# Storing each expert's outputs by index to the rows of its pairs, and the last seven tiles in one branch

## The chip, the cores and the metric

The kernel runs on one core of a Trainium2 chip. The metric is the device time of one execution in microseconds (us). Engines are named as in the profile: PE (TensorE, matrix products), DVE (VectorE), ACT (ScalarE), POOL (GpSimd) and SP (SyncE, which only issues DMAs here). POOL issues DMAs too, and all those that go by a list of row numbers (indirect ones) are issued by it.

## What is computed

One decoder layer over 4 sequences of 512 tokens with 512 features, in f32:

```
x = x + attn (layernorm(x))     # Mamba: projections, conv, selective scan, out_proj
x = x + xattn(layernorm(x))     # two int8 SmoothQuant linears per sequence
x = x + ffn  (layernorm(x))     # mixture of experts
```

The change lies in the last line. Of 16 experts each token takes its two best, with weights `topw` that add to one:

```
topw, sel = top_k(softmax(x @ gate_w.T), 2);  topw /= topw.sum(-1)
combine[t, sel[t]] = topw[t]
hmid = silu(x @ w1[e].T) * (x @ w3[e].T)              # 128 wide
moe_out = sum over e of combine[:, e] * (hmid @ w2[e].T)
out = moe_out + sigmoid(x @ shared_gate.T) * shared(x)
```

So each token has two pairs (token, expert), and its result is the shared part plus two weighted rows.

## The kernel before, in words

**Order of the work.** Most of the time goes to the scan: 256 units, each with `bu` on POOL (L726), `da` on ACT (L724), the scan itself and `h` on DVE (L733, L739) and sums on PE (L751). Beside the units of later batches run the `backs`: for each sequence out_proj, layernorm (L377 to L395), the two quant linears (`amx` and `s` on POOL at L927 to L930) and `moe_front` (layernorm, router, shared expert). The sequences form two groups of two, and `experts` (L1240) does the routed part of one group. Group 0 begins beside the scan of the last sequence, group 1 when that sequence has been routed, after the scan.

Every piece of such work is a generator that yields what it waits for. While the kernel is written out, a planner, `Pace` (L133 to L245), keeps a model of each engine's time with fixed costs and lets a piece go on beside the scan only if the model says that nothing of the scan is held up (`clear`, L222). After the scan the piece goes first whose wait is ready first (`run`). Each engine then executes its own instructions strictly in the order written out; so does SP's and POOL's queue with their DMAs.

**One group of experts.** A group has 1024 tokens, thus T = 8 token tiles of 128 and 2048 pairs. `sort` (L1354) orders the pairs by expert and lays them out in tiles of 128 rows, each tile of one expert only. At most NS = 2T + 16 - 1 = 31 tiles are needed; 16 always are (`sure`), 24 are called `likely`, and the number for the given data is in `count`. `sort` leaves three index tables: `tok`, the token row of each place in a tile (out of bounds where it is empty), `wrow`, the weight rows of each tile's expert, and `pos`, the place of each token's two pairs.

`expert_tiles` (L1475) goes through the tiles. `load` has POOL gather the tile's rows, `xs` (L1507, 256 KB), and its expert's weights, `wx` (L1263, 768 KB). `steps` then are: four transposes on PE (L400), a copy to `xT` on ACT (L1529), 16 products (L1538), Tanh on ACT (L1544), two operations on DVE (L411, L1548), the product with w2 (L1553), a copy to `ys` on ACT (L1557), and a plain store of the tile by SP to its own 128 rows of `y_d` (L1561). Up to 8 tiles are loaded ahead after the scan, 2 during it; three are in work at a time. `load` of tile s+8 is written out when tile s has ended.

For tiles that may not be needed, `part` (L1483) puts each single step into a branch of the engine that does it. For tiles 16 to 23 only the two products are in a branch, with a small product as the other way; for tiles 24 to 30 every step but the loads is, on every engine, SP's store among them. The branch reads `count`:

```
if s < sure or s < likely and out is None: yield; return
...
with self.tc.If(counts[engine] > s) as real: yield
```

**The sums.** At the end of a group, for each of the 8 token tiles: SP fetches the rows of the residual with the shared part, `xr4` (L1278, 256 KB; for group 1 all eight are fetched by `some` when the last tile's loads are written out), POOL gathers the two `yg` by `pos` from `y_d` (L1301), DVE multiplies by `topw` and adds, twice (L1311), and SP stores to `out` (L1318). Rows of `y_d` above the likely tiles are filled from `x` once, during the scan (`first_experts`, L1672), since nothing else may have written them.

Of the kernel before, what the change touches and what calls it, by code (L numbers as in the profile page):

```python
# [8 lines left out]
F32 = mybir.dt.float32  # L9
# [10 lines left out]
P = 128  # L20
B = 4
L = 512
# [110 lines left out]
class Pace:  # L133
# [23 lines left out]
    def take(self, ins):  # L157
        outs = [x for x in ins.outs if hasattr(x, "bass_ap")]
        ins_ = [x for x in ins.ins if hasattr(x, "bass_ap")]
        e = str(ins.engine).rsplit(".", 1)[-1]  # L160
        if not outs or e not in self.engine:
            return
        n = 1
        for _, size in list(outs[0].ap)[1:]:
            n *= size
        kind = type(ins).__name__
        keys, outs_ = [self.key(x) for x in ins_], [self.key(x) for x in outs]
        start = max([self.engine[e]] + [self.written.get(k, 0) for k in keys])
        if e != "SP":
            start = max([start] + [max(self.written.get(k, 0), self.read.get(k, 0)) for k in outs_])  # L170
        if "DMA" in kind:
            end = start + (950 if e == "Pool" else self.FIXED[e])
            size = 1
            for _, x in outs[0].ap:
                size *= x
            self.queue = max(self.queue, end) + size * 4 / 220
            self.engine[e], done = end, max(self.queue, end + 1000) + 1000
        else:
            if e == "PE":
                cost = 40 + self.product(n / 4 if outs[0].ap[0][1] == CH else n, ins_[0].dtype == F32)  # L180
            else:
                cost = self.FIXED[e] + n * self.EACH[e] * (2 if getattr(ins, "is_tensor_tensor_scan", False) else 1)
            if e == "Activation" and kind == "InstActivation":
                table = self.TABLES.get(str(ins.func).rsplit(".", 1)[-1], self.table)
                if table != self.table:
                    cost += 1280
                    self.table = table
            self.engine[e] = start + cost
            done = self.engine[e] + self.HOP
        for k in keys:  # L190
            self.read[k] = max(self.read.get(k, 0), done)
        for k in outs_:
            self.written[k] = done
# [76 lines left out]
class Kernel:  # L270
    def __init__(self, ctx, tc, args):
        self.tc, self.nc = tc, tc.nc
        for name, ap in args.items():
# [35 lines left out]
        self.y_d = [  # L309
            self.dram.tile([(2 * n * NT + E - 1) * P, DM], F32, name=f"y_d{i}") for i, (_, n) in enumerate(GROUPS)  # L310
        ]
# [7 lines left out]
        self.started = set()  # L319
# [920 lines left out]
    def experts(self, sb, group, bank, ahead):  # L1240
# [13 lines left out]
        pos = sb.tile([P, T, 2], U32, name=f"pos{group}", bufs=1)  # L1254
# [17 lines left out]
        yield from self.sort(sb, bank, group, fixed, pos, tok, wrow, count, lambda: [weights(s) for s in range(ahead)], min(ahead, 3))  # L1272
        y_d = self.y_d[group]
        xr = {}
# [11 lines left out]
        yield from self.expert_tiles(group, place, bank, NS, tok, ws, count, weights, some, self.xn_d[group], y_d)  # L1286
# [5 lines left out]
        def load(t):  # L1292
            if t not in xr:
                fetch(t)
            if sb is self.last:
                both = sb.tile([P, 2, DM], F32, name="yg", tag="wx")
                ys[t] = [both[:, i, :] for i in range(2)]
            else:
                ys[t] = [self.us.tile([P, DM], F32, name="yg", tag="u") for i in range(2)]
            for i in range(2):  # L1300
                nc.gpsimd.indirect_dma_start(  # L1301
                    out=ys[t][i],
                    out_offset=None,
                    in_=y_d,
                    in_offset=bass.IndirectOffsetOnAxis(ap=pos[:, t, i : i + 1], axis=0),
                )
            return *ys[t], xr[t]
# [15 lines left out]
    def sort_fixed(self, sb, group):  # L1323
# [18 lines left out]
        tokf = iota("tokf", [[P, T]], 0, 1)  # L1342
# [11 lines left out]
    def sort(self, sb, G, group, fixed, pos, tok, wrow, count, first_weights, few):  # L1354
# [78 lines left out]
        nc.vector.tensor_copy(pos, posf)  # L1433
# [10 lines left out]
        for t in range(0, T, 2):  # L1444
# [17 lines left out]
                tokf[:, t : t + 2].rearrange("p (a b q) -> p a b q", b=1, q=1).to_broadcast([P, 2, 2, NS]),  # L1462
# [8 lines left out]
        nc.vector.tensor_add(tok, pk, none)  # L1471
# [3 lines left out]
    def expert_tiles(self, group, place, bank, NS, tok, ws, count, weights, some, xn_d, y_d):  # L1475
# [4 lines left out]
        counts = {}  # L1480

        @contextmanager
        def part(s, engine, out=None, n=1):  # L1483

            if s < sure or s < likely and out is None:
                yield
                return
            if engine not in counts:  # L1490
                counts[engine] = engine.value_load(count)
            with self.tc.If(counts[engine] > s) as real:
                yield
                inside = list(nc.cur_bb.bb.instructions)
            if s < likely:
                with real.Else():
                    some = self.identb.unsqueeze(1).to_broadcast([P, n, P])
                    nc.tensor.matmul(
                        out.rearrange("p (n q) -> p n q", n=n), self.identb, some, start=True, stop=True
                    )  # L1500
            self.pace.update()
            for ins in inside:
                self.pace.take(ins)
# [14 lines left out]
        def steps(s):  # L1518
# [5 lines left out]
            with part(s, nc.tensor):  # L1524
                self.transposes(tp, xs[s], NK)
            yield ACT, tp
            xT = sb.tile([P, NK, P], F32, name="xT", bufs=few)
            with part(s, nc.scalar):
                nc.scalar.copy(xT, tp)  # L1529
# [4 lines left out]
            with part(s, nc.tensor, ph.rearrange("p i q -> p (i q)"), 2):  # L1534
# [8 lines left out]
            with part(s, nc.scalar):  # L1543
                nc.scalar.activation(h, ph[:, 0, :], AF.Tanh, scale=0.5)  # L1544
            yield h
            with part(s, nc.vector):
                self.swish(h, h, ph[:, 0, :])
                nc.vector.scalar_tensor_tensor(h, h, 0.5, ph[:, 1, :], ALU.mult, ALU.mult)  # L1548
# [3 lines left out]
            with part(s, nc.tensor, py, NK):  # L1552
                nc.tensor.matmul(py, h, w[:, W2:], start=True, stop=True)  # L1553
            yield ACT, py
            y = sb.tile([P, DM], F32, name="ys", bufs=min(ahead, 6))
            with part(s, nc.scalar):
                nc.scalar.copy(y, py)  # L1557
            bank.done(py)
            yield SP, y
            with part(s, nc.sync):  # L1560
                nc.sync.dma_start(y_d[s * P : (s + 1) * P, :], y)  # L1561
# [3 lines left out]
        while ended < NS:  # L1565
            while loaded < NS and loaded - ended < place()[1]:
                load(loaded)
                loaded += 1
            self.done.add(("begun", group))
            if loaded == NS:  # L1570
                some()
# [7 lines left out]
            if one.over:  # L1579
                going.remove(one)  # L1580
                ended += 1

# [84 lines left out]
    def first_experts(self):  # L1667
        yield lambda: "pool" in self.done

        for y_d, (_, n) in zip(self.y_d, GROUPS):  # L1670
            rest = y_d[(2 * n * NT + E // 2) * P :, :]
            self.nc.sync.dma_start(rest, self.x.rearrange("b l d -> (b l) d")[: rest.shape[0], :])  # L1672
            yield SP
# [135 lines left out]
```

## Time and profile before

| What | Value |
|---|---|
| five runs: median, lowest, highest | 1635.13, 1628.33, 1638.32 us |
| the profiled execution: its own time | 1630.59 us |
| its span in the trace | 1628.9 us |
| mean granted PE clock | 0.849 |
| busy: PE, DVE, POOL, ACT | 1196.2, 1197.1, 1125.5, 941.1 us |
| `bu` on POOL (L726) | 256 times 2358 ns |
| `wx` gathers on POOL (L1263) | 62 times 1023 ns |
| `xs` gathers on POOL (L1507) | 62 times 1038 ns |
| `yg` gathers on POOL (L1301) | 32 times 1032 ns |
| additions on DVE (L1311) | 32 times 752 ns |
| `y_d` stores by SP | 48, of 256 KB each |

The span runs from the first to the last instruction of the profiled execution; its own time is 1.7 us longer. That execution is one of its own, so its time is compared with the runs' median only as a whole. No engine is busy for more than 73% of the span, because the stages have different limits: the scan runs until about 1338 us, the last sequence's quant linears until about 1441, then come its router, the sort of group 1 and the group's tiles, and from about 1586 the sums. The 48 stores are 24 in each group: the branches of tiles 24 to 30 were not taken, in either group.

A group of instructions is named by line, engine and "out<-in". A wait is named by what ended it; "issue" is time in which an engine waited for nothing that the profile shows. The copies to `ys` (L1557) mark the ends of tiles.

### The profile page before, as it was taken

The page shows a single profiled execution, that of the slowest core. Times are in us where ns is not written, and L with a number is a line of the kernel's source. Part 1 is how long each engine was busy: PE and PEld are TensorE (multiplying, and loading weights), DVE is VectorE, ACT ScalarE, POOL GpSimd, SP SyncE. Part 2 cuts the span into 40 slices and gives each one's busy share as a digit, 9 for nine tenths or more (in the row PEclk, how much of TensorE's full clock was granted, in tenths as well). Part 3 has the DMA queues.
Part 4 walks back from the last instruction along what each step waited for, and adds up shares of the span by engine and source line. Part 5 has one row for each costly group of instructions (what it writes and reads, how often), then busy time and mean ns, then how long its engine had stood idle before and what let it go on. Part 6 is the DMA issues. An engine that isn't in the chain of part 4 may idle for free. (4 is left out here: it accounts for less than half of the span.)

```text
span 1628.9 us, 15724 instructions
## 1 busy us (share of the span) xinstructions
PE 1196.2 (73%) x4544; PEld 584.3 (36%) x4552; DVE 1197.1 (73%) x1256; ACT 941.1 (58%) x1592; POOL 1125.5 (69%) x935
## 2 busy tenths in 40 slices
PE   5867777557865767899867885856767799868990
PEld 2323222112332323333423432334434346644770
DVE  4588999898868888788787888977788863444312
ACT  3386776755667778555797753377676323630240
POOL 1079899886768888676887965687778654316564
PEclk9977888779887887999878888987787999968995
DMA  5476555675233655666344559665556557257976
GB/s 199 146 184 131 131 113 113 127 191 115 80 85 79 137 123 151 172 181 169 82 99 118 158 125 274 161 179 142 143 147 184 142 189 265 78 194 272 362 277 219
DMA packets 109658, 262.22 MB, mean 161 GB/s; under 512 B 16192, under 2 KB 20416, under 8 KB 109504
## 3 DMA queue, kind: packets, MB, share of 16 engines
q1 hardware_dynamic: 93120, 204.50, 47.9%
q0 software_dynamic: 16448, 56.65, 9.8%
q8 instruction: 40, 0.66, 0.2%
q14 instruction: 50, 0.41, 0.1%
HBM read 168.55 MB, written 45.88 MB: 132 GB/s over the span
## 5 line engine op out<-in xcount | busy, mean ns | idle before, releaser
L726 POOL TENSOR_TENSOR bu<-bc,rep 128x1024 f32<-128x1024 f32 x256 | 602.1, 2358 | 178.4 <-DVE da L733 133.2
L733 DVE TENSOR_TENSOR_SCAN da<-da,bu 128x1024 f32<-128x1024 f32 x256 | 586.2, 2290 | 88.5 <-POOL bu L726 55.6
L724 ACT ACTIVATE da<-rep,a_sb 128x512 f32<-128x512 f32 x512 | 352.6, 690 | 249.2 <-DVE h L739 221.4
L739 DVE TENSOR_TENSOR h<-da,bc 128x1024 f32<-128x1024 f32 x256 | 312.3, 1220 | 18.9 <-PE py L751 8.7
L751 PE MATMUL py<-h,sel 128*32 128x512 f32 x1024 | 163.8, 679 | 49.0 <-DVE h L739 49.0
L1263 POOL DMA_INDIRECT wx<-in_wexp,wrow x62 | 63.4, 1023 | 73.1 <-PE bank L1553 25.1
L502 POOL TENSOR_TENSOR u<-u,tap 128x511 f32<-128x511 f32 (+2 forms) x72 | 91.2, 1266 | 17.0 <-ACT tap L498 14.7
L446 PE MATMUL bank_a<-xnT,win 128*128 128x512 f32 x176 | 96.7, 701 | 8.3 <-ACT tap L498 5.6
L446 PE MATMUL bank_g<-xnT,win 128*128 128x512 f32 x184 | 90.8, 639 | 7.4 <-ACT tap L498 4.2
L751 PEld LDWEIGHTS py<-h,sel 128*32 128x32 f32 x1024 | 30.9, 118 | 159.9 <-issue 82.0
L1507 POOL DMA_INDIRECT xs<-xn_d,tok x62 | 64.4, 1038 | 21.0 <-issue 15.1
L446 PE MATMUL bank_b<-xnT,win 128*128 128x512 f32 x120 | 60.5, 651 | 13.0 <-ACT sp_r L681 10.9
L446 PEld LDWEIGHTS bank_a<-xnT,win 128*128 128x128 f32 x176 | 39.1, 231 | 60.8 <-issue 50.0
L446 PEld LDWEIGHTS bank_g<-xnT,win 128*128 128x128 f32 x184 | 36.6, 206 | 59.8 <-issue 43.7
L1538 PE MATMUL bank<-xT,wx 128*128 128x128 f32 x384 | 49.5, 288 | 1.9 <-ACT xT L1529 1.9
L695 POOL TENSOR_TENSOR sp_e<-sp_e,dd 128x512 f32<-128x512 f32 x31 | 39.4, 1272 | 16.4 <-ACT dd L690 16.2
L1538 PEld LDWEIGHTS bank<-xT,wx 128*128 128x128 f32 x384 | 47.4, 202 | 5.3 <-ACT xT L1529 2.9
L1301 POOL DMA_INDIRECT yg<-y_d,pos x32 | 33.0, 1032 | 18.6 <-DMA y_d<-ys 9.1
L1311 DVE SCALAR_TENSOR_TENSOR xr<-yg,topw,xr 128x512 f32<-128x512 f32 x32 | 23.8, 752 | 28.0 <-DMA yg<-y_d,pos 27.6
L411 DVE SCALAR_TENSOR_TENSOR hs<-hs,bank 128x128 f32<-128x128 f32 x24 | 6.9, 286 | 51.0 <-ACT hs L1544 49.7
L446 PEld LDWEIGHTS bank_b<-xnT,win 128*128 128x128 f32 x120 | 24.7, 213 | 48.7 <-issue 30.2
L693 ACT ACT_TABLE_LOAD x32 | 41.1, 1283 | 0.5
(434 smaller groups left out, 2387.2 us busy)
## 6 DMA issues: line engine op xcount, KB each, us to landing
rep<-dd SPq DMA_DIRECT2D x128, 512.0 KB, 8.1
win<-in_win SPq DMA_DIRECT2D x64, 256.0 KB, 3.0
x<-xr SPq DMA_DIRECT2D x48, 256.0 KB, 2.0
xr<-x SPq DMA_DIRECT2D x48, 256.0 KB, 4.7
y_d<-ys SPq DMA_DIRECT2D x48, 256.0 KB, 4.2
bc<-rows_d SPq DMA_DIRECT2D x32, 256.0 KB, 5.7
gz_d<-gz SPq DMA_DIRECT2D x32, 256.0 KB, 3.4
gzl<-gz_d SPq DMA_DIRECT2D x32, 256.0 KB, 3.5
```

Of the source, the lines that this page charges most:

```text
L446: nc.tensor.matmul(pj, win[:, k, :], xnT[:, k, :], start=(k == 0), stop=(k == NK - 1))
L502: nc.gpsimd.tensor_add(u[:, j:], u[:, j:], v[j][:, j:])
L693: nc.scalar.activation(w, w, AF.Ln)
L695: ew.tensor_sub(e, e, du)
L724: nc.scalar.activation(da[:, i, :], rep[:, i, 0, :], AF.Exp, scale=self.a_sb[:, q, g : g + 1])
L726: nc.gpsimd.tensor_mul(bu, st["bc"][0, g].unsqueeze(1).to_broadcast([P, NP, L]), rep[:, :, 1, :])
L733: self.nc.vector.tensor_tensor_scan(daf, daf, buf, 0.0, ALU.mult, ALU.add)
L739: self.nc.vector.tensor_mul(h, st["da"].pop((c, n)), st["bc"][1, g].unsqueeze(1).to_broadcast([P, NP, L]))
L751: nc.tensor.matmul(py[q * CH : (q + 1) * CH, :], self.sel, st["h"][c, g, q // NP][:, q % NP, :], start=False, stop=(g == NG - 1),)
L1263: nc.gpsimd.indirect_dma_start(out=ws[s], out_offset=None, in_=self.wexp, in_offset=bass.IndirectOffsetOnAxis(ap=wrow[:, s : s + 1], axis= ...
L1507: nc.gpsimd.indirect_dma_start(out=xs[s], out_offset=None, in_=xn_d, in_offset=bass.IndirectOffsetOnAxis(ap=tok[:, s : s + 1], axis=0), bo ...
L1538: nc.tensor.matmul(ph[:, i, :], w[:, o : o + P], xT[:, k, :], start=(k == 0), stop=(k == NK - 1))
```

## The change

The change has five parts.

1. The sort now computes with the number of a pair (token times 2, plus 0 or 1) where it computed with the token. Its end makes two tables from it: `pair` (out of bounds where a place is empty) and `tok` by halving. `pos` is not kept. Five small DVE operations stand where one stood.
2. `y_d` is smaller, with a row for each pair. A tile's result is stored by POOL with an indirect DMA, to the rows of `pair`; places out of bounds are not stored. The scatters are declared independent of one another.
3. The sums read plain rows: SP loads `yg`, for group 1 both rows of 128 tokens in one DMA of 512 KB, for group 0 in two of 256 KB. Each of these loads waits for all scatters of its group. POOL's gathers go.
4. The loop goes over the 24 likely tiles. The other seven stand after it in one branch of all engines, loads included, and the fetch of `xr4` comes after that. Of the branches on single steps those around the products of tiles 16 to 23 stay.
5. The fill of `y_d` from `x` goes, and the planner's model knows the scatter (950 ns of POOL, 256 KB of queue).

In the order written out after the change, POOL has 24 scatters more per group, 14 loads of tiles 24 to 30 and 16 gathers fewer. After the scan its order per tile is the scatter of tile s, then `xs` and `wx` of tile s+8. Beside the scan stand 11 scatters, and 2 loads fewer. At the end of the branch that isn't taken POOL waits for all its DMAs.

```diff
@@ Pace.take
+        scattered = "DMA" in kind and e == "Pool" and outs_[0][0].startswith("y_d")
+        if e != "SP" and not scattered:
...
+            if scattered:
+                size = P * DM
@@ __init__
-            self.dram.tile([(2 * n * NT + E - 1) * P, DM], F32, name=f"y_d{i}") for i, (_, n) in enumerate(GROUPS)
+        self.y_d = [self.dram.tile([2 * n * L, DM], F32, name=f"y_d{i}") for i, (_, n) in enumerate(GROUPS)]
@@ experts
+        y_of = y_d.rearrange("(t p i) d -> t p i d", p=P, i=2)
...
-            for i in range(2):
-                nc.gpsimd.indirect_dma_start(
-                    out=ys[t][i],
-                    out_offset=None,
-                    in_=y_d,
-                    in_offset=bass.IndirectOffsetOnAxis(ap=pos[:, t, i : i + 1], axis=0),
-                )
+            loads = [(both, y_of[t])] if sb is self.last else [(ys[t][i], y_of[t, :, i, :]) for i in range(2)]
+            for to, of in loads:
+                ins = nc.sync.dma_start(to, of)
+                for other in self.scattered[y_d.tensor.name]:
+                    info = mybir.DependencyInfo(mybir.DependencyClass.Sync, mybir.DependencyReason.DATA)
+                    self.tc.add_manual_dep(ins.ins, other.name, info, reason="all pairs are there")
@@ sort_fixed and sort
-        tokf = iota("tokf", [[P, T]], 0, 1)
+        tokf = iota("tokf", [[2 * P, T], [1, 2]], 1, 2)
...
-        nc.vector.tensor_copy(pos, posf)
...
-        nc.vector.tensor_add(tok, pk, none)
+        nc.vector.tensor_scalar(ex, pk, 0.5, float(4 * T * P), ALU.is_lt, ALU.mult)
+        nc.vector.scalar_tensor_tensor(pair, pk, -1.0, ex, ALU.add, ALU.add)
+        nc.vector.tensor_scalar(ex, pk, -1.5, 0.5, ALU.add, ALU.mult)
+        nc.vector.tensor_scalar(ex, ex, MAGIC, -MAGIC, ALU.add, ALU.add)
+        nc.vector.scalar_tensor_tensor(tok, ex, 0.0, none, ALU.max, ALU.add)
@@ expert_tiles
-            yield SP, y
-            with part(s, nc.sync):
-                nc.sync.dma_start(y_d[s * P : (s + 1) * P, :], y)
+            yield POOL, y
+            ins = nc.gpsimd.indirect_dma_start(
+                out=y_d,
+                out_offset=bass.IndirectOffsetOnAxis(ap=pair[:, s : s + 1], axis=0),
+                in_=y,
+                in_offset=None,
+                bounds_check=2 * rows - 1,
+                oob_is_err=False,
+            )
+            for other in self.scattered.setdefault(y_d.tensor.name, []):
+                self.tc.declare_no_dep(ins.ins, other, reason="a pair has one place")
+            self.scattered[y_d.tensor.name].append(ins.ins)
...
-        while ended < NS:
-            while loaded < NS and loaded - ended < place()[1]:
+        while ended < likely:
+            while loaded < likely and loaded - ended < place()[1]:
...
-            if loaded == NS:
-                some()
...
+        yield "PE", bank.free
+        with self.tc.If(nc.values_load(count) > likely):
+            for s in range(likely, NS):
+                load(s)
+                for _ in steps(s):
+                    pass
+        self.pace.update()
+        some()
@@ first_experts
-        for y_d, (_, n) in zip(self.y_d, GROUPS):
-            rest = y_d[(2 * n * NT + E // 2) * P :, :]
-            self.nc.sync.dma_start(rest, self.x.rearrange("b l d -> (b l) d")[: rest.shape[0], :])
-            yield SP
```

## The prediction

> **What bounds the kernel now.** I read the program from its end. The chain of waits (start, length, what ran) reaches back over the last 37 us only, and it is the part that the change rebuilds:
>
> ```profile
> 1591.45 7.17 DMA y_d<-ys
> ...
> 1598.78 0.70 issue
> 1599.48 0.28 POOL yg L1301
> ...
> 1606.18 1.02 POOL yg L1301
> 1607.20 0.30 issue
> 1607.50 4.43 DMA yg<-y_d,pos
> ...
> 1618.84 0.94 POOL yg L1301
> 1619.78 0.30 issue
> 1620.09 4.45 DMA yg<-y_d,pos
> ...
> 1624.63 0.75 DVE xr L1311
> ```
>
> The last expert tile is stored in 7.17 us, behind the eight fetches of 256 KB that SP issues from 1587.44 on. Then 16 gathers follow one another on POOL, each about 1.00 us of work and 0.30 us of "issue": 1.30 us for 256 KB. The last one lands after 4.45 us, one addition of 0.75 us follows, and the span ends 3.5 us after that with the last out store.
>
> Next I read busy time by stretch, for what lies ahead of the tail (columns: us, then busy us of PE, its loads, DVE, ACT, POOL; PE clock, DMA share, GB/s):
>
> ```profile
> 1500.00:1550.00 50.00, 50.00 (x289) 36.19 (x288) 20.96 (x43) 13.56 (x31) 29.66 (x29) 1.00 0.95 346
> 1550.00:1600.00 50.00, 35.37 (x238) 27.96 (x236) 7.30 (x26) 17.60 (x40) 27.43 (x28) 0.89 0.70 257
> 1600.00:1629.00 29.00, 0.00 (x0) 0.00 (x0) 12.02 (x16) 0.00 (x0) 16.46 (x16) 0.50 0.69 217
> ```
>
> PE is full until the last tiles and the DMA engines nearly so; afterwards PE is idle and no engine is full. The copies of `ys` come three by three, 9.4 us apart, so a tile costs 3.13 us there; the last three run from 1585.97.
>
> Last the scan, by the waits of POOL from 1080 to 1338 (us in all, times, longest):
>
> ```profile
> POOL bu L726 <- DVE da L733: 30.4, 16, 5.3
> POOL wx L1263 <- PE py L751: 7.8, 1, 7.8
> ...
> POOL wx L1263 <- PE bank_a L1553: 3.7, 1, 3.7
> ```
>
> In these 258 us DVE is busy 202.8, POOL 187.2, PE 183.1. DVE and POOL wait for each other; POOL has more slack, but it stalls whenever an indirect DMA ahead of `bu` waits for a buffer.
>
> **Part 1, the tail.** Removed: 16 gathers on POOL. Added: a scatter per tile on POOL in place of SP's store, and eight plain loads of 512 KB on SP that wait for all 24 scatters. In the changed order POOL does scatter(s), xs(s+8), wx(s+8) for each tile: 3 × 1.30 = 3.9 us against PE's 3.13, while there is something to load. The scatter of tile 3 can go at the copy of 1532.6; 13 tiles (3 to 15) later it is 1532.6 + 13 × 3.9 = 1583.3. Eight scatters without loads remain: + 8 × 1.3 = 1593.7. The weights of tile 20 come 2 to 3 us late for PE, which POOL's own lag hides. The last scatter lands 2.9 us later (the median of xs from 1580 on): 1596.6 where the last store landed at 1598.6. SP's loads start 0.7 us behind it (the issue piece above): 1597.3. The first 512 KB take 4.2 us (the median of the `ws` loads, same size): 1601.5. DVE then needs 16 × 0.756 = 12.1 us: 1613.6, and the end comes 3.5 us later: 1617.1, **-12 us**. DMA allows that: 4.2 MB of loads and 2.1 MB of out stores at the 346 GB/s of the first row above take 18.2 us, up to 1615.5 or a little after.
>
> The scatter is in no trace of before. Nearest rows: xs, which moves as many rows of as many bytes the other way, 0.94 to 1.50 us. With 1.5, POOL is 24 × 0.5 = 12 us later and the gain is gone; at 0.9 and without lag PE's end decides, and the gain is 15. I take 1.00, where nearly all indirect DMAs lie.
>
> A rule speaks against this part. The rows say that a 256 KB gather costs POOL 1.30 us and that in the tail DMA moves 217 GB/s, against 346 in the tile stage: so the issuing engine was the limit. The Trainium skill, "DMA: Bandwidth & Descriptors", section "Issuing engines are not separate DMA queues", says that another issuing engine saves only the sequencer's time, which is usually small beside the transfer. By that rule the tail would stay at 217 GB/s (6.3 MB in 29 us), this term would be nil and the sum below +10 instead of -2. The same page, section "Issuing engine by pattern", gives simple stores to Sync and indirect ones to GpSimd, and the change turns 48 of the former into the latter; the price of that is in parts 1 to 3.
>
> **Part 2, the scan.** Eleven scatters come into POOL's order beside the units of the last batch, and two loads fewer: 9 × 1.3 = 11.7 us of POOL, against the 30.4 us in which it waits for DVE. So the work itself could be hidden. But a scatter waits at POOL's head for its `ys`, with xs, wx and `bu` queued behind it; before, SP took that wait. The row for such a wait is the 7.8 and the 3.7 us in which wx blocked POOL for a buffer of a tile. Bounds: 0 (each `ys` is ready, slack takes the rest) and +15 (nothing hidden, and one more stall of 3.7). I take **+5**, nearer to the slack row, since the planner places scatters late. SP loses the stores, whose waits for `ys` held its queue for 133.3 us from 1190 on; behind them stood the loads of `rep`, for which `bu` waited 2.3 us once in this window: 0, at most -2. The gathers of group 0 become plain loads on SP: 16 × 1.3 us leave POOL between 1492 and 1513, where PE is full: 0.
>
> **Part 3, layernorm and first quant of the last batch.** Before, POOL idles 10.94 us ahead of its first `ln_scale` at 1363.01, the last ends at 1371.6, and `amx` runs at 1377.2. After, four scatters, each followed by xs and wx, stand ahead of `ln_scale`, and six DMAs more ahead of `amx`. ACT copies the `ys` in question only around 1366.8, so by my estimate `ln_scale` runs from 1370.8 to 1376 and `amx` around 1385. That is 8 us on the chain which leads to the sort of group 1. PE is busy 48.4 of 50 us from 1350 to 1400, with tiles, so a part may be made up. Bounds 0 and +10; I take **+7**, near the row of the idle time.
>
> **Part 4, branches.** The seven conditional tiles had one branch per step on each engine. In the second quant (1419 to 1441) waits for the queue of L1492 amount to 14 us over all engines, about 5 along one chain. After, one count load and one branch on each engine remain, and POOL waits there until all its DMAs have landed: 2 to 7 us if it meets the chain (landings of xs: 2.1 to 9.3). Bounds -7 and +1; **-3**. The rest: five small DVE operations on 128x31 instead of one in the sort, +0.8; dropping the pos copy and the 2 × 1792 KB fill at 1000 (landed in 11.7 us, beside the scan), 0, at most -1; one tile more after the scan, 0 to +3, PE's 3.13, hidden in its gaps: 0.
>
> **Sum:** -12 + 5 + 7 - 3 + 1 = -2 us. The profiled execution took 1630.59, so 1628.6; its time lies 4.5 below the runs' median of 1635.13, so about **1633** against that median.
>
> **Rivals.** A, my case (42%): the tail's gain is nearly eaten by POOL's in-order waits; own range 1626 to 1640. B (25%): the waits are covered. For it: the 30.4 us of slack, POOL's 10.94 us idle ahead of `ln_scale`, and PE, which needs the same tile work before and after. Tail -12, scan 0, layernorm +3, branches -3, sort +1: -11, **1624**. C (28%), the other side: the scatter at the head of POOL's queue holds `bu` in the scan and `ln_scale` and `amx` after it. For it: DVE already waits for `bu`, the chain of the last batch leads to all of group 1, and nothing after 1480 can give time back, since PE is full there. Scan +14, layernorm +9, sort +1, tail -12, branches -2: +10, **1645**. It decides from the point where scan and layernorm together exceed 14 us. D (5%): the change doesn't do what it says: the tail stays DMA-bound at 217 GB/s, or scatters of 1.5 us make POOL the bound of the tile stage; tail 0, the rest as in A: +10, 1645 too.
>
> **Chances.** This measurement can tell about 0.3%, 4.9 us. A: faster 0.15, same 0.22, slower 0.05. B: faster 0.24, same 0.01. C: slower 0.26, same 0.02. D: slower 0.04, same 0.01. Together 0.39, 0.26, 0.35. The range takes in B with 7 us more (a tail at -15, branches at -7) and C with 5 more (scan at +15, one tile more): 1617 to 1650.
>
> **What would show it.** Right: POOL's scatters at 1.0 us plus 0.3; the last scatter landing some 20 us ahead of the span's end, where the last store landed 30 ahead; DVE's 16 additions back to back; `ln_scale` 5 to 8 us later against the end of the scan; `bu` behind scatters that wait for ACT. Wrong: scatters of 1.5 us, additions that wait for `yg`, or PE waiting for wx through the tile stage. The estimate of part 3 is the weakest: if the tile work that PE does earlier is worth as much as the chain loses, B holds.

## The result and the profile after

| | before | after |
|---|---|---|
| median of all runs | 1636.05 us (94 runs) | 1638.96 us (52 runs) |
| lowest, highest | 1628.24, 1642.41 | 1634.46, 1647.47 |
| profiled execution, its span | 1630.59, 1628.9 | 1639.75, 1638.0 |
| mean granted PE clock | 0.849 | 0.843 |

The ratio after to before is 1.0024, with a 95% interval of 1.0016 to 1.0031: slower, by about 3 to 5 us. The two profiled executions lie 9.2 us apart, because that of before is 5.5 below its median and that of after 0.8 above. A part of this can be seen: up to the first steps of the routed work both programs hold the same instructions, and there after is late by 3.2 us already. I set the clocks of the two traces at that place and read what each stage takes from there (each column is one execution):

| Stage (its end) | before | after | difference |
|---|---|---|---|
| to the start of scan unit 192 (same instructions) | 985.4 | 988.6 | +3.2 |
| scan, on to the start of the last unit | 339.1 | 355.4 | +16.3 |
| layernorm and first quant (`amx`) of the last batch | 52.7 | 59.6 | +6.9 |
| on to the second quant's `amx` | 42.2 | 38.6 | -3.6 |
| router and sort, to group 1's first `xs` transpose | 78.1 | 75.6 | -2.5 |
| tiles of group 1, to the end of the last `ys` copy | 89.9 | 92.8 | +2.9 |
| tail, to the end of the span | 41.4 | 27.4 | -14.0 |

The tail is what the change was expected to make of it. Its chain of waits in the profile after (start, length, what ran):

```profile
1609.86 7.54 DMA y_d<-ys,pair
...
1618.63 5.48 DMA yg<-y_d
1624.15 0.76 DVE xr L1313
1624.93 1.43 DVE xr L1313 x2
...
1632.18 0.75 DVE xr L1313
```

One landing of a scatter, one plain load, and then additions without a gap, where before POOL's gathers stood one after another. By stretch (PE, loads of PE, DVE, ACT, POOL, clock, DMA share, GB/s):

```profile
1517.00:1610.00 93.00, 88.88 (x539) 65.92 (x537) 29.61 (x71) 31.95 (x72) 53.06 (x53) 1.00 0.76 278
1610.00:1638.00 28.00, 0.00 (x0) 0.00 (x0) 11.41 (x16) 0.60 (x2) 3.80 (x4) 0.53 0.68 251
```

DVE does its 16 additions in 11.41 us of 28, and DMA moves 251 GB/s, where it was 217 in the tail before.

What is lost behind the scan stands on POOL. Its order around the layernorm of the last batch (start, length, line, operation; in brackets the idle time ahead and what ended it):

```profile
1372.20 0.99 POOL L1265 DMA_INDIRECT wx<-in_wexp,wrow  x1 [0.31 <-issue]
1385.15 1.03 POOL L1558 DMA_INDIRECT y_d<-ys,pair  x1 [11.96 <-ACT ys L1555]
1386.48 1.03 POOL L1510 DMA_INDIRECT xs<-xn_d,tok  x1 [0.30 <-issue]
1387.82 0.99 POOL L1265 DMA_INDIRECT wx<-in_wexp,wrow  x1 [0.31 <-PE bank_g L808]
1388.88 0.26 POOL L391 TENSOR_SCALAR ln_scale<-ln_mv 128x1 f32<-128x1 f32 x1
```

POOL stands idle for 11.96 us until a tile's `ys` is there, and `ln_scale` waits behind it without need: its first `ln_mv` was there at 1381.6, 7.3 us earlier, and it starts at once when the three DMAs are issued. Near the end of the scan a scatter waits ahead of `bu` in the same way:

```profile
1328.99 1.06 POOL L1558 DMA_INDIRECT y_d<-ys,pair  x1 [7.06 <-ACT ys L1555]
...
1332.70 4.66 POOL L728 TENSOR_TENSOR bu<-bc,rep 128x1024 f32<-128x1024 f32 x2
```

But DVE, which takes `bu`, does not wait for it there: all its longer pauses from 1300 on are for PE, and one for ACT. Over the whole scan stage it is much the same. DVE is busy for 279.8 of its 339.1 us before and for 280.1 of 355.4 after, so what is lost is idle time of DVE. Its waits for `bu` and for PE's sums `py` in the stage, before (us in all, times, longest):

```profile
DVE da L733 <- POOL bu L726: 15.7, 6, 5.7
DVE u L773 <- PE py L751: 1.1, 1, 1.1
```

and after:

```profile
DVE da L735 <- POOL bu L728: 17.3, 8, 5.5
DVE h L741 <- PE py L753: 8.5, 2, 8.0
DVE u L775 <- PE py L753: 6.9, 4, 2.8
```

The waits for `bu` grow by 1.6 us, those for `py` by 14.3. The longest of them comes 50 us before the first scatter is issued (1095.1). PE and DVE there:

```profile
1025.55 10.04 PE L808 MATMUL bank_g<-wout,u 128*128 128x512 f32 x16
1035.52 7.11 PE L808 MATMUL bank_a<-wout,u 128*128 128x512 f32 x16
1043.61 1.92 PE L753 MATMUL py<-h,sel 128*32 128x512 f32 x16
```

```profile
1044.71 1.23 DVE L741 TENSOR_TENSOR h<-da,bc 128x1024 f32<-128x1024 f32 x1 [7.95 <-PE py L753]
```

Two blocks of out_proj (L808) stand ahead of `py`; before, `py` (1031.19) ran between them (1020.11 and 1033.04). So the planner has laid out another order, from the group's sort on, and by these waits most of what after loses in the scan goes through that order. What changed it, no run shows by itself: it changes ahead of any scatter, and e10 and e13 below, which keep the fill of `y_d`, also keep the order of before, so the missing fill is the likely cause.

### The profile page after: what moved, and what is told of

Read it like the earlier page. It is cut to its first block, busy times and chain, and to the rows that moved or that the text cites. A ratio compares the mean times of both kernels' runs of the same rounds, so it can differ in the third digit from the quotient of the medians.

```text
span 1638.0 us, 15481 instructions
## 1 busy us (share of the span) xinstructions
PE 1200.7 (73%) x4544; PEld 589.7 (36%) x4552; DVE 1196.6 (73%) x1262; ACT 941.5 (57%) x1592; POOL 1111.8 (68%) x923
## 5 line engine op out<-in xcount | busy, mean ns | idle before, releaser
L1558 POOL DMA_INDIRECT y_d<-ys,pair x48 | 49.6, 1034 | 97.8 <-ACT ys L1555 88.1
L448 PE MATMUL bank_a<-xnT,win 128*128 128x512 f32 x176 | 92.8, 676 | 8.9 <-ACT tap L500 6.1
L1265 POOL DMA_INDIRECT wx<-in_wexp,wrow x48 | 48.8, 1017 | 29.7 <-issue 11.3
L1510 POOL DMA_INDIRECT xs<-xn_d,tok x48 | 49.2, 1026 | 19.1 <-issue 12.8
L808 PE MATMUL bank_g<-wout,u 128*128 128x512 f32 x80 | 44.5, 716 | 14.9 <-ACT tap L500 6.2
L448 PEld LDWEIGHTS bank_b<-xnT,win 128*128 128x128 f32 x120 | 24.7, 213 | 48.5 <-issue 31.2
L703 POOL TENSOR_TENSOR dd<-dd,u 128x512 f32<-128x512 f32 x31 | 39.4, 1272 | 1.3
L699 POOL TENSOR_TENSOR sp_e<-sp_e,sp_r 128x512 f32<-128x512 f32 x31 | 39.4, 1270 | 1.3
L701 POOL TENSOR_TENSOR dd<-sp_e,sp_w 128x512 f32<-128x512 f32 x31 | 39.3, 1268 | 1.1
```

The source lines that it names most:

```text
L448: nc.tensor.matmul(pj, win[:, k, :], xnT[:, k, :], start=(k == 0), stop=(k == NK - 1))
L808: nc.tensor.matmul(po[t], st["u"][c][:, t * P : (t + 1) * P], wout[c], start=(c == part[0]), stop=(c == part[-1]),)
L1265: nc.gpsimd.indirect_dma_start(out=ws[s], out_offset=None, in_=self.wexp, in_offset=bass.IndirectOffsetOnAxis(ap=wrow[:, s : s + 1], axis= ...
L1510: nc.gpsimd.indirect_dma_start(out=xs[s], out_offset=None, in_=xn_d, in_offset=bass.IndirectOffsetOnAxis(ap=tok[:, s : s + 1], axis=0), bo ...
L1558: ins = nc.gpsimd.indirect_dma_start(out=y_d, out_offset=bass.IndirectOffsetOnAxis(ap=pair[:, s : s + 1], axis=0), in_=y, in_offset=None, ...
```

## The experiments

The theory at first (W): the tail's gain is real, and group 0's scatters give it back, beside the scan and ahead of the layernorm. It came apart into two that had to be told apart: Q, the scatter's wait for its `ys` at the head of POOL's queue, and P, POOL's time of 1.33 us for each scatter. Rivals were the planner's new order (R in e10, O) and the branches (B).

All kernels are one source with switches for each group (0, 1): SCAT for the scatter, its sort and the plain loads of the sums; ONE for the one branch; LAG for the number of tiles by which a scatter is issued later; TWICE for the number of scatters. With all switches off it is the kernel before, with SCAT and ONE on the kernel after, instruction for instruction. The `y_d` of a group with plain stores is filled from `x`; where a group scatters, a spare tensor takes its fill in e1, e7 to e9 and e13 to e18, and nothing does in e2, e3, e6, e11 and e12. The edits are shown as the switches' values. Kernels that ran together had runs of before beside them on the same chip, and a ratio is to these. The stages of all the traces, in us, cut as above:

| | ratio (95%) | scan | to amx 1 | to amx 2 | to tiles | tiles | tail |
|---|---|---|---|---|---|---|---|
| e5 before again | 0.9995 (0.9981 to 1.0010) | 339.5 | 52.8 | 42.2 | 78.1 | 104.5 | 40.7 |
| e6 after again | 1.0062 (1.0038 to 1.0086) | 355.7 | 59.7 | 38.5 | 75.4 | 114.4 | 26.5 |
| e1 group 1 only | 1.0027 (1.0006 to 1.0047) | 340.5 | 52.7 | 43.5 | 76.6 | 120.5 | 26.0 |
| e7 the same again | 1.0016 (0.9998 to 1.0034) | 341.2 | 52.7 | 42.3 | 76.3 | 123.5 | 26.5 |
| e2 group 0 only | 1.0189 (1.0159 to 1.0220) | 352.4 | 70.2 | 48.5 | 74.5 | 97.2 | 40.9 |
| e3 scatter only | 1.0240 (1.0210 to 1.0270) | 357.0 | 59.6 | 49.1 | 78.5 | 124.0 | 34.4 |
| e4 one branch only | 0.9917 (0.9893 to 0.9941) | 339.5 | 52.8 | 42.2 | 74.8 | 99.5 | 35.0 |
| e15 the same again | 0.9906 (0.9877 to 0.9935) | 341.3 | 52.8 | 42.3 | 74.7 | 95.4 | 35.0 |
| e8 one branch, group 1 scatters | 0.9994 (0.9978 to 1.0010) | 340.1 | 52.8 | 43.6 | 73.5 | 123.3 | 25.3 |
| e9 e8, lag 2 | 0.9942 (0.9917 to 0.9967) | 342.2 | 52.7 | 43.6 | 73.5 | 118.3 | 27.7 |
| e10 sort only | 1.0007 (0.9991 to 1.0024) | 342.9 | 52.8 | 42.2 | 78.1 | 102.9 | 42.2 |
| e11 after, lag 1 | 0.9972 (0.9954 to 0.9990) | 359.2 | 48.1 | 39.3 | 74.0 | 109.3 | 26.2 |
| e12 group 0 twice | 1.0370 (1.0344 to 1.0396) | 350.7 | 122.5 | 33.1 | 74.6 | 115.2 | 26.9 |
| e13 order of e4 | 1.0041 (1.0023 to 1.0060) | 354.8 | 54.4 | 43.8 | 72.9 | 116.2 | 26.0 |
| e14 e13, lag 1 and 2 | 0.9997 (0.9980 to 1.0014) | 361.8 | 47.6 | 38.8 | 76.4 | 110.4 | 27.4 |
| e16 e13, lag 1 and 2, order kept | 0.9984 (0.9960 to 1.0007) | 351.5 | 55.4 | 45.6 | 73.1 | 93.2 | 27.2 |
| e17 e13, group 0 twice, order kept | 1.0109 (1.0072 to 1.0146) | 366.3 | 56.9 | 43.7 | 72.9 | 94.1 | 27.9 |
| e18 e4, group 1 scatters, lag 3 | 0.9931 (0.9908 to 0.9954) | 343.3 | 52.7 | 43.6 | 73.5 | 97.4 | 25.4 |

Stages of traces from different chips agree up to group 1's tiles (before: 339.1 and 339.5 us of scan, then 52.7 and 52.8), but not in the tiles: before has 89.9 in the first trace and 104.5 in e5. Tile stages are therefore compared only within e1 to e15 (three chips), or between the first two traces and e16 to e18. Each trace is one execution: those whose scan has the instructions of before up to one small one (before, e1, e4, e5, e7, e8, e9, e15, e18) need 339.1 to 343.3 us for it, so a smaller difference than 4 us between two scans tells nothing. Medians of before were 1649.29 beside e1 to e4, 1652.64 beside e5 to e8, 1651.12 beside e9 to e12, 1651.17 beside e13 to e15 and 1636.41 beside e16 to e18.

### Halves of the change (e1 to e8)

e1 and e7, the change in group 1 alone (before has both switches off):

```diff
-SCAT, ONE = (False, False), (False, False)
+SCAT, ONE = (False, True), (False, True)
```

> Group 1 as after the change (scatter, plain loads, one branch), group 0 as before; a spare tensor takes the fill of the second y_d, so that the scan's instructions are those of before. Theory W (the loss comes from group 0's scatters, which wait for ys in POOL's order beside the scan and ahead of the layernorm of the last batch; the tail's gain is real): scan, layernorm and quants as before, tile stage +3, tail -14: 11 us less than before, about 1625. Rival T (the tail's gain exists only because the profiled tail differs from run to run): -3 or less, 1633 to 1638. Rival L (POOL's three DMAs per tile cost the tile stage more when it starts early): -5, 1631.

> As e1, now beside a trace of before from the same chip. Theory W: the tile stage within 4 us of before's, tail -14, so 8 to 11 us less. Theory S (scatters themselves slow the tile stage of group 1, by 15 to 20 us, and eat the tail): the tile stage 15 us longer than before's here, total 0 to +5.

Neither W nor L, and not T either: the tail is 14 us shorter than e5's both times, but the tile stage took 16 and 19 us longer, so nothing is gained. That is theory S of e7.

e2, the change in group 0 alone:

```diff
+SCAT, ONE = (True, False), (True, False)
```

> Group 0 as after the change, group 1 as before. Theory W: scan +8 to +16, layernorm and first quant +7, branches -4, no gain in the tail: 12 to 19 us more than before, 1648 to 1655. Rival R (the scan's loss is the accident of one profiled execution): +3 to +7, 1639 to 1643.

W in sign, but larger: +1.9%, most of it behind the scan, 17 us up to the first `amx` and 6 more up to the second. Its order beside the scan is neither that of before nor that of after (one of the two fills stays), so it is no clean half of the change: e1 and e2 together are above e6.

e3, the scatter without the one branch, and e4, the one branch without the scatter:

```diff
+SCAT, ONE = (True, True), (False, False)     # e3
+SCAT, ONE = (False, False), (True, True)     # e4, e15
```

> The change without its last part: both groups scatter, but tiles 24 to 30 keep one branch for every step on every engine, the scatter's on POOL too, and their loads. Theory W: the branches cost the second quant 4 us, as in the step of the prediction, and POOL 14 more loads per group: 3 to 8 us more than after, 1642 to 1647. Rival B (the one block's wait of POOL for all its DMAs costs as much as the branches): as after, 1637 to 1641.

> Before with the last part alone: plain stores by SP and gathers, but tiles 24 to 30 in one block in one branch of all engines. Theory W: second quant -4, and in the tail POOL no longer has loads of tiles that are not there ahead of the gathers, which is worth 0 to 4: 4 to 8 us less than before, 1628 to 1632. Rival B: 0, 1636.

Here the change falls apart into a gain and a loss. The one branch alone is worth 0.8 to 0.9%, more than either theory gave; the scatter alone costs 2.4%, also more than either. Both together have 1.0062 (e6), so the parts don't simply add up. Against e5, e4 shows where its gain lies: 3.3 us ahead of the tiles, 5 us in them (9 in e15; all on different chips, so this part is rough), and 5.7 in the tail. The last is a queue: before, eight fetches of `xr4` stood on SP ahead of the last store, which took 7.17 us to land; with the block behind the loop they come after it. Its chain in e4:

```profile
1598.15 2.49 DMA y_d<-ys
...
1601.41 0.96 POOL yg L1318
```

e5 and e6, before and after again, to have their traces from the chip of e7 and e8:

> The kernel before again, instruction for instruction, so that a trace of it exists from the chip on which its neighbours run: the stages of e1 to e4 differ from the first two traces in places where no instruction was changed (group 1's tile stage took 95.7 to 124 us there against 88.4 and 92.2), so either the chip or the code of these kernels is slow there. If the chip: the tile stage takes about 100 us here too and idle 'issue' time shows on PE, DVE and ACT. If the code: 88 us, as in the first trace.

> The kernel after again, beside before on one chip. Theory W: ratio 1.002 to 1.004 as on record, scan +10 to +16, tail -14. Theory J (each If splits the code of all engines, and jumping between the pieces costs time that depends on the chip): where before is at 1649, after with a third of the jumps is at 1640 or less; where before is at 1636, after is at 1639.

It is the chip: before itself needs 104.5 us for the tiles there. After's scan is again 16.2 us longer and its way to the first `amx` 6.9, as in the first pair; the tile stage is 10 longer instead of 3, and the ratio is above W's. Theory J's numbers do not fit, after is not at 1640 there.

e8, both groups with one branch, group 1 alone scatters:

```diff
+SCAT, ONE = (False, True), (True, True)
```

> Both groups with one branch for tiles 24 to 30; group 0 stores plainly by SP and gathers, group 1 scatters and loads plainly. Theory W: e4's gain (ratio 0.992) and the tail's: 18 to 24 us less than before, ratio 0.985 to 0.989. Theory S: no more than e4, ratio 0.992 to 1.000.

Theory S: e4's gain is gone. Against e4 the tail is 9.7 us shorter and the tile stage 23.8 longer. In it POOL waits for `ys` (us in all, times, longest):

```profile
POOL y_d L1610 <- ACT ys L1593: 34.7, 10, 8.4
```

### Waits or time (e9 to e12)

e9 takes these waits away in group 1, e11 in both groups of after:

```diff
 SCAT, ONE = (False, True), (True, True)      # e9
+LAG = (0, 2)
 SCAT, ONE = (True, True), (True, True)       # e11
+LAG = (1, 1)
```

> As e8, but each scatter of group 1 is issued two tiles later, behind the loads for the tiles after it, so that POOL's loads do not wait behind a scatter that waits for its ys (35.6 us of POOL in e8's tile stage). Theory Q (this in-order wait makes e8's tile stage 24 us longer than e4's): the tile stage falls from 122.7 to 100 to 105 us, the tail stays short, ratio 0.985 to 0.991. Rival P (three DMAs of 1.33 us per tile on POOL are themselves the limit): the tile stage stays above 113 us, ratio 0.995 to 1.000.

> After, with every scatter issued one tile later, in both groups. Theory Q: POOL's 12 us of waits for ys beside the scan and those of the tile stage (51 us) go for the most part: scan +4 to +8 instead of +16, tile stage 5 to 10 us shorter, ratio 0.990 to 0.998 where after has 1.006. Rival P: as after, 1.004 to 1.008.

Both are faster than without the lag, by 0.5 and 0.9%, so the waits cost time. e11's ratio is Q's, and 48.1 us to the first `amx` are less than before's; but its order is another one, and its scan is no shorter: 359.2. e9's ratio lies between Q's and P's, and its tile stage, 118.3, is P's (that execution took 1653.54, at the upper end of its runs, whose median is 1642.87).

e10, the sort's new arithmetic in group 0 alone, with a pair table that nobody reads:

```diff
+            if group == 0:
+                self.pair_too = sb.tile([P, NS], U32, name=f"pair{group}", bufs=1)
...
-        if SCAT[group]:
+        if SCAT[group] or group == 0:
```

> Before, with the new arithmetic of the sort in group 0 alone (pair numbers, five operations at its end), whose pair table nobody reads; stores, gathers and branches are those of before. Only the order in which the planner lays the sort's steps among the scan's units can differ. Theory W: ratio 1.000 to 1.001. Rival R (the loss in the scan is the planner's other order from the sort on, not the scatter): scan +5 to +14, ratio 1.003 to 1.008.

W: no difference in the time. The scan, 342.9 against e5's 339.5, lies within the spread of traces with this order. The sort isn't the cause.

e12, group 0's scatters twice, the second to a spare tensor:

```diff
+TWICE = (2, 1)
```

> After, with each scatter of group 0 issued a second time, to a spare tensor: 24 more DMAs on POOL, 11 of them beside the scan, at the same places. Theory Q: their 1.33 us each fall into POOL's slack for the most part, +0 to +6 beside after. Rival P (POOL's time itself is what the scan lacks): +14 in the scan and more behind it, +14 to +25 beside after.

Neither: +51 us beside e6, none of it in the scan. The planner had seen the doubled DMAs and laid out another order: `ln_scale` of the last batch stands between the last tiles there, each time behind scatters, and its last one behind a wait for the landing of a second scatter (`y_x`):

```profile
1455.35 0.24 POOL L401 TENSOR_SCALAR ln_scale<-ln_mv 128x1 f32<-128x1 f32 x1 [3.79 <-DMA y_x<-ys,pair]
```

So it takes 122.5 us to the first `amx` instead of 59.7. What POOL's time costs the scan, this run can't tell, since the order is another; nor can e11.

### With the order held fixed (e13 to e18)

e13 lets the planner take a scatter for the store that it replaces and keeps the fills, to a spare tensor, so that PE's order is e4's to the last instruction (against e6, the fills left out):

```diff
+        if scattered:
+            e = "SP"          # in the planner's model only
...
-                yield POOL, waiting[0][1]
+                yield SP, waiting[0][1]
```

> As after, but the planner's model takes each scatter for the plain store by SP that it replaces, and a spare tensor takes the fills, so that PE's order is that of e4 to the last instruction and POOL's differs only by the scatters, the gathers gone and the sort's iota. Theory O (the scan's 16 us come from the order that the planner chooses when the scatter is modelled as work of POOL): scan +0 to +5 instead of +16, total 1.000 or below where after has 1.006. Rival Q (the scatter in POOL's order, waiting for its ys, is what costs the scan): scan +12 to +25, total 1.006 or more.

Rival Q over O by the scan, which is 15.3 us longer than e4's in the same order and 13.5 longer than e15's, on e13's chip; by the ratio, 1.0041, between the two. So the planner's new order isn't needed for a loss of this size, and without it the scan loses by another way than after does. The order of e4 is the better one ahead of the tiles, where e13 loses only 1.6 us up to the first `amx`.

e14 was meant as e13 with lags, but its waits gave the planner another order again; e15 is e4 again:

> As e13, with scatters one tile late in group 0 and two tiles late in group 1. Theory O and Q together (order of e4 and no waits for ys on POOL): scan +0 to +3, tile stage as in e9, short tail: ratio 0.985 to 0.992. Rival P (POOL's three DMAs per tile): 0.995 to 1.002.

> e4 again, beside e13 and e14 on one chip, since PE's order is the same in all three: 0.990 to 0.994. If the scatter is worth having at all in the tail, e14 is below it; if not, above.

e14 misses what O and Q gave, with the longest scan but one; with its other order it tells no more than e11. e15 repeats e4.

e16 and e17 change one thing on POOL each and leave the order of every other instruction as in e13: e16 issues group 0's scatters one tile later and group 1's two (no waits of POOL for `ys` beside the scan), e17 issues group 0's twice in a row (no more waits, twice the time):

```diff
+LAG = (1, 2)        # e16, the planner sees the store at its old place
+TWICE = (2, 1)      # e17, the second one unseen by the planner
```

> As e13, order of PE and of every other instruction unchanged, but on POOL each scatter of group 0 stands one tile later and each of group 1 two tiles later, where its ys is long there. Theory Q (a scatter's wait for its ys at the head of POOL's queue is the cost): the scan loses +2 to +7 instead of +15, total 5 to 12 us below e13, ratio 0.994 to 1.000. Rival P (POOL's 1.33 us per scatter): the scan stays at +11 to +15, ratio 1.000 to 1.004.

> As e13, with each scatter of group 0 issued once more, to a spare tensor, right behind itself, unseen by the planner, so that every other instruction keeps its place: 12 more DMAs on POOL beside the scan and 12 behind it, without one more wait for a ys. Theory Q: scan +15 to +19 (e13 has +15), total at most 10 us above e13. Rival P: scan +26 to +30, total 15 to 25 us above e13.

The scan, against e4's 339.5: e13 +15.3, e16 +12.0, e17 +26.8. For e16 and e17 that is P's range, but against e18's 343.3, from their own chip, e16 has +8.2, between Q and P. The ratios are not P's either: e16's, 0.9984, is Q's, and e17's, 0.7% above e13's, lies between Q and P. DVE's waits for `bu`, from 986 to 1352, in e15, e13 and e17:

```profile
DVE da L744 <- POOL bu L737: 14.5, 6, 5.7
```

```profile
DVE da L747 <- POOL bu L740: 24.7, 8, 8.4
```

```profile
DVE da L750 <- POOL bu L743: 39.6, 12, 11.0
```

And POOL's waits for DVE, of the same three:

```profile
POOL bu L737 <- DVE da L744: 42.5, 21, 5.8
```

```profile
POOL bu L740 <- DVE da L747: 36.9, 20, 5.8
```

```profile
POOL bu L743 <- DVE da L750: 34.5, 18, 5.8
```

DVE's wait grows by 10.2 and 14.9 us, while POOL's slack shrinks by only 5.6 and 2.4. In e13 some 25 of the 36.9 us lie before the first scatter, at 1094, or between 1290 and 1322, where no scatter stands.

How much of e13's loss is the wait (Q) and how much POOL's time (P) can be read against e15, unit by unit. Two scatters waited for their `ys`, 3.86 us at 1221 and 6.71 at 1331, and the units behind them fall back by 3.2 and 3.3 us: 6.5 of the 13.5. Most of the other 7 arise at scatters that waited for no `ys`. In e17, 12 further DMAs of 1.31 us (15.7 us) add 11.5 us to e13's scan. So both count, roughly half and half; each number is from single traces.

e16 doesn't price POOL's time by itself, as it was meant to, because its waits moved to ACT. In e16 a `ys` is free again only when the later scatter has landed. ACT's waits for that, and DVE's for `da` and `bu`:

```profile
ACT ys L1603 <- DMA y_d<-ys,pair: 24.9, 3, 13.3
```

```profile
DVE da L755 <- ACT da L746: 15.1, 4, 10.7
DVE da L755 <- POOL bu L748: 14.8, 8, 4.9
```

DVE waits for `bu` no longer than without scatters (14.5 in e15), but 8 us longer for ACT.

e18 keeps e4 and its order, and scatters in group 1 alone, three tiles late:

```diff
 SCAT, ONE = (False, True), (True, True)
+LAG = (0, 3)        # order of e4 kept
```

> e4, its order unchanged, with group 1 alone scattered, three tiles late, and its sums read as plain rows. Theory Q: tile stage 2 to 8 us longer than e4's 98.9 (POOL has a third DMA per tile but never waits for ys), tail 9 us shorter: ratio 0.985 to 0.991, below e4. Rival P: tile stage 10 us longer or more, ratio 0.991 to 0.996.

The ratio, 0.9931, lies in P's range and above e4's 0.9917, but its interval reaches into Q's. POOL's waits for `ys` in the tile stage are nearly gone (4.6 us in all, e8 had 34.7):

```profile
POOL wx L1288 <- PE bank_b L1599: 5.0, 1, 5.0
POOL y_d L1622 <- ACT ys L1603: 4.6, 5, 3.3
```

The stage has 97.4 us against 89.9 of the first trace of before, with the tail at 25.4. e4, e9, e11, e15 and e18 are all faster than both kernels. Which of e4 and e18 is the faster one stays open: they ran on chips with different tile stages. e18 and e16 did run on one chip, and differ in group 0's scatters, which e18 lacks, and in the lag of group 1: the medians are 1624.50 and 1634.09, so group 0's scatters cost about 10 us there even with POOL's waits for `ys` gone (ACT waits in their place, as said).

## Why the prediction was right or wrong, step by step

The range and the size of the time held; the sign did not: -2 us was forecast and the runs give +2.9 in the medians. By its own time the profiled pair gives +9.2, of which 3.2 arise ahead of any changed instruction, so about +6.

- **Scan, the step that failed.** The prediction gave it +5, since "the work itself could be hidden" in the 30.4 us in which POOL waits for DVE. It is +16.3 and +16.2 in the two pairs of traces, above even the upper bound of 15. Two things were wrong in it. First, it took the order of the other work as given, and put the dropped fill at 0, at most -1: in after the order differs from the sort on, and DVE's waits for `py` grow by 14.3 us, those for `bu` by 1.6. Second, the slack does not hide the scatters: with the order of e4 (e13) the scan still loses 13.5 us against e15, about half of it by the waits for `ys` and half by POOL's time, and 12 more DMAs of 15.7 us add 11.5 (e17). The slack was read as a sum, but POOL and DVE wait in turns, and most of it lay where no scatter stands. That the total stayed inside the range is in part luck, since no term stood for PE's order. What the new order would cost without scatters, no run shows.
- **Layernorm and first quant:** +7 forecast, +6.9 measured twice. The mechanism is that of the prediction, a scatter ahead of `ln_scale` that waits 11.96 us, of which `ln_scale` loses 7.3. It hangs on the order, too: in e13 POOL waits 9.4 us for `ys` in this stage, and the stage is only 1.6 us longer than e4's.
- **Branches:** -3 forecast. e4 has -3.3, between the second `amx` and the tiles instead of inside the second quant. But the prediction missed what the block does further on: 5 us in the tiles and 5.7 in the tail of e4.
- **Tail:** -12 forecast, from the end of PE's work with POOL's lag in it; tiles and tail together measure -11.1 (131.3 to 120.2). The last scatter landed some 20 us ahead of the span's end, as forecast. The lag came as worked out: POOL issues three DMAs in 3.97 us (3.9 forecast) from 1540 on, and the last scatter went out at 1613.7, with the tiles' last `ys` at 1610.6. The split between the parts was wrong: 5.7 us of the tail belong to the branch block (e4), and the scatter adds 9 to 10 (e4 against e8).
- **Scatter on POOL:** 1.00 us forecast, 1.034 measured over 48, with 0.30 of issue behind it. (The range of 0.94 to 1.50 that the prediction gives for xs is misread: xs took 0.99 to 1.51, and 0.94 is of `yg`.)
- **Sort and fill:** +1 forecast; e10, the sort alone, shows nothing in the time. The missing fill comes with the new order (see the scan).
- **Rival C** had the sizes: scan +14, layernorm +9, from the point where both exceed 14 us. They came to 23, but of its mechanism, a scatter that holds `bu` and `ln_scale`, after shows the second and hardly the first; the way on to the tiles, 6.1 us shorter where C had 1, kept the total at +6 by this pair of traces. It had 28%, my own case 42%.
- **The rule** that another issuing engine saves only the sequencer's time, usually small beside the transfer (the Trainium skill, "DMA: Bandwidth & Descriptors", section "Issuing engines are not separate DMA queues"), would have made the tail's term nil. The traces say otherwise for POOL's gathers: 1.30 us of POOL each for 256 KB, and the tail is 9.7 us shorter without them (e8 against e4). The same page's table in "Issuing engine by pattern" gives simple stores to Sync, and there the runs agree: a plain store on SP costs POOL nothing, and e4, which keeps it, has 0.9917 where after has 1.0062 (e6).

Open: why the tile stage is 24 us longer with scatters (e8) than without (e4) on those chips, but only 3 us longer in the first pair of traces. POOL's in-order waits are a small part: e9 was 0.5% faster without most of them. More shows on ACT: its waits ahead of `hs` and `xT` for which the trace names no cause ("issue" or "remote") come to 39.7 us in e8 and 38.1 in e9, but 8.4 in e4 and 13.3 in e15. In the first pair and in e16 to e18 there are none, with scatters or without. What makes them grow with the scatters is not shown.

## What to carry to other kernels

Slack of an engine that works in turns with another is no budget: price a moved instruction at its full time unless the trace shows the engine idle at the very place where it will stand (here 11.5 of 15.7 us came through). A store that waits for its data belongs on a queue with nothing urgent behind it, or later in its queue, where its data is there (one tile's lag gave 0.9% back, e11 against e6); but then its buffer is held longer, and another engine may wait for that (24.9 us of ACT in e16). Compare the order of every engine before and after ahead of pricing anything: here it changed 50 us before the first moved instruction. And measure the parts of a change by themselves: here a gain of 0.8% and a larger loss stood in one change and nearly cancelled.

## What the runs showed of the hardware

The same program needed 1636 us on some chips and 1649 to 1653 on others, and the traces of before put all of it behind 1498 us, in group 1's tiles: up to the first of them the two agree within 0.4 us, and then the tiles take 89.9 us (DMA share 0.84) or 104.5 (0.74). On the slower chip ACT stands still for over 2 us ahead of a `hs` once in three tiles or so. Before, in the first trace:

```profile
1546.17 0.28 ACT L1544 ACTIVATE hs<-bank 128x128 f32<-128x128 f32 x1 [1.17 <-PE bank L1538]
1547.96 0.28 ACT L1544 ACTIVATE hs<-bank 128x128 f32<-128x128 f32 x1 [1.51 <-PE bank L1538]
```

The same place in e5, the same instructions:

```profile
1556.45 0.28 ACT L1579 ACTIVATE hs<-bank 128x128 f32<-128x128 f32 x1 [3.78 <-issue]
1557.31 0.28 ACT L1579 ACTIVATE hs<-bank 128x128 f32<-128x128 f32 x1 [0.58 <-remote]
```

Nothing in the trace says what it waits for; the cause wasn't found. A ratio measured on one chip need not be that of another: after stands at 1.0024 in the result and at 1.0062 beside e5.
